# A gated windowed attention kernel: first loads over two queues, idle transposes at the outset, transposes placed beside maxima, last reciprocals placed one tile earlier

## The chip, the cores and the metric

The kernel runs on one core of one Trainium2 chip. The metric is the device time of one execution in microseconds; of several runs the median counts. Five engines share the work: TensorE (PE in the profile, its weight loads PEld), VectorE (DVE), ScalarE (ACT), GpSimd (POOL) and SyncE (SP), which here only issues DMA transfers. ScalarE issues DMA too. Each engine takes its instructions in order and waits on semaphores for the others.

## The reference

For 8 batches of 1024 tokens with 512 features: a layer norm, a windowed attention with 16 heads of 32 features, a gate from a layer of signs, and a residual sum.

```python
xn = _layernorm(x)
q, k, v = proj(xn, Wq, bq), proj(xn, Wk, bk), proj(xn, Wv, bv)
scores = q @ k^T / sqrt(32)
im = arange(1024) % 256
scores = where(im[:, None] >= im[None, :], scores, -1e30)
s = softmax(scores) @ v @ Wo^T + bo
w = (weights >= 0) * 2 - 1
g = silu(clip((xn @ w^T) * scale + bias, -100, 100))
out = x + s * g
```

The lines from `q, k, v` on are shortened; all is float32.

## The kernel before

The tokens are loaded in an order in which the four windows alternate (`tokens`, L127), so that a tile of 128 tokens holds 32 places of each window. The mask is then triangular over tiles, and about half of all tiles of scores is left out.

The work goes by batch `b` and by group `g` of four heads. One group takes nine steps (`NQ`), and a step has two score quads, each four PSUM banks wide, that share one buffer. `probs_quad` (L571) writes scores with keys in rows (lines L577, L588, L599), less the maximum of each query, and ScalarE makes probabilities of them (L612). `maxima_quad` (L494) writes scores of the next group with queries in rows (L501, L515), and VectorE takes maxima of them (L528). Between the two quads TensorE is given other work to fill its time: in the place after a `probs_quad` it also multiplies the last step's probabilities with the values (`attend_quad`, L625). POOL adds probabilities up over tiles (`add_probs`, L643); TensorE sums them over keys (`sum_keys`, L666, or at the end `sum_quad`, L687), ScalarE copies the sums (L661), and VectorE takes reciprocals, 128 columns at a time (`invert`, L700), and multiplies (`normalise_heads`, L704).

The filling work is projections (`product`, L339 to L371, whose matmuls are all L351: q, k, v and the output o), gate tiles (`gate_work`, y_ps, L426 to L449), and turns: transposes by TensorE, four 128x128 blocks into one PSUM bank, which ScalarE or VectorE then copies out. Turned are the normalised tokens of the next batch (`turn` in `norm_work`, L313 to L324), the weights (`turn_weight`, L241; wo's are turned in the third group of the first batch, by words `W` of `OPENING`), and the maxima (`shift_rows`, L552). Products and turns share two PSUM banks (`bank`, L121). An open product holds one of the two until its last chunk is copied out.

The order is planned by hand-written strings (`STEADY`, `OPENING`, `CLOSING`, L787 to L804), one word for each piece, made into `Work` items with costs in microseconds and a test of whether they are ready. `Beside.fill` (L919) takes from this list in each of two places of a step, as much as the place wants: after the score quad of the probabilities up to about 1.2, and after the maxima's up to 2.35 or 2.45 or an even share. Work marked `turn` is allowed once in a place (`turns=1`) or not at all, and is put at the place's end (`edge`). The loop over steps is L1053 to L1140.

At the outset (L154 to L175) all loads are issued: four token tiles of the first batch on SyncE's queue, wk in two halves of 512 KB and three biases on ScalarE's, then four more token tiles, wq, wv, the signs' weights, three rows and wo on SyncE's. The loads share eight semaphores in rotation, so from the ninth on each is issued only when the one eight before it has landed. L993 to L1027 follow: 24 idle transposes into a bank that nobody reads, the turns of wk with four copies by ScalarE, the bias turned, statistics (L285, L286), scale (POOL, L292, L293), normalisation (L305) and turns of four token tiles, the first product of k, constants and statistics of four more tiles on VectorE, wq's turns and the first product of q.

At the end (L1143 to L1162) the output tiles 4, 5, 6, 7, 0, 1, 2, 3 of the last batch are made. Each takes 16 matmuls (L351), two operations of VectorE (L722, L723), one of POOL (L724) and a store. For tiles 0 to 3 a reciprocal and a product of VectorE come first. The last tile goes by `last_output` (L733).

Of the kernel before, what the change touches and what calls it, by code (L numbers as in the profile page):

```python
# [9 lines left out]
F32 = mybir.dt.float32  # L10
# [6 lines left out]
P = 128  # L17
B = 8
L = 1024
D = 512  # L20
# [3 lines left out]
NT = L // P  # L24
NC = D // P
NH = P // DK
# [47 lines left out]
def tile_gated_window_attention(  # L74
# [16 lines left out]
    nc = tc.nc  # L91
# [35 lines left out]
    def tokens(a, b, it):  # L127
        return a[b].rearrange("(w m) d -> m w d", w=NW)[it * MT : (it + 1) * MT]
# [1 line left out]

    xt = {}

    def load_x(b, it):

        where, tag = (vpool, "v") if (b, it // 4) == (0, 1) else (xpool, "x")
        t = where.tile([P, D], F32, tag=tag, name=f"x_{b}_{it}")
        nc.sync.dma_start(t, tokens(x, b, it))
        xt[b, it] = t


    staged = {}

    def fetch_weight(name, src, tiles, queue):

        staged[name] = [t[:, o, :] for t in tiles for o in range(t.shape[1])]
        n = D // len(tiles)
        for i, t in enumerate(tiles):
            queue.dma_start(t, src[i * n : (i + 1) * n, :].rearrange("(o p) d -> p o d", p=P))

    def chunks(where, tag, name):  # L150
        t = where.tile([P, NC, D], F32, tag=tag, name=name)
        return [t[:, 0:2, :], t[:, 2:4, :]]

    for it in range(4):  # L154
        load_x(0, it)
    fetch_weight("wk", wk, chunks(probs, "p", "wk_st"), nc.scalar)
    bias_r = temp("bias_r")[0 : 3 * NC, 0:P]
    for i, src in enumerate((bq, bk, bv)):
        nc.scalar.dma_start(bias_r[i * NC : (i + 1) * NC, :], src.rearrange("(c p) -> c p", p=P))
    bias_c = const.tile([P, 3 * NC], F32, name="bias_c")  # L160
    bq_c, bk_c, bv_c = (bias_c[:, i * NC : (i + 1) * NC] for i in range(3))
    for it in range(4, NT):
        load_x(0, it)
    fetch_weight("wq", wq, chunks(probs, "p", "wq_st"), nc.sync)
    fetch_weight("wv", wv, chunks(total, "total1", "wv_st"), nc.sync)
    fetch_weight("fw", fw, chunks(total, "total0", "fw_st"), nc.sync)
    rows = {}
    for name, src in (("fscale", fscale), ("fbias", fbias), ("bo", bo)):
        t = const.tile([P, D], F32, name=f"{name}_r")
# [1 line left out]
        rows[name] = t  # L171
    fetch_weight(
        "wo", wo,
        [heads.tile([P, 1, D], F32, tag="a0", name=f"wo_st_{o}") for o in range(NC)], nc.sync,
    )  # L175


# [50 lines left out]
            self.early = False  # L228


    wT = {}
    copies = [0]

    def evacuate(dst, src):
# [6 lines left out]
    def turn_weight(name):  # L241


        def turn(c):
            if c == 0:
                wT[name] = const.tile(
                    [P, NC, D], F32R if name == "fw" else F32, name=f"{name}T"
                )
            dst = wT[name]
            if name == "wk" and c % 2:  # L250

                ps = ps_a.tile([P, 512], F32, tag="av", name=f"wkT_{c}")
            else:
                ps = bank(f"{name}T_{c}")
            for o in range(NC):
                nc.tensor.transpose(
                    ps[:, o * P : (o + 1) * P], staged[name][o][:, c * P : (c + 1) * P], ident
                )
            if name == "fw":

                sg = temp(f"sign_{c}")
                nc.vector.tensor_scalar(sg, ps, 0.0, 2.0, ALU.is_ge, ALU.mult)
                nc.vector.tensor_scalar(dst[:, c, :], sg, -1.0, None, ALU.add)
            elif name == "wo":

                nc.scalar.mul(dst[:, c, :], ps, 0.5)
            elif name == "wk":
                nc.scalar.copy(dst[:, c, :], ps)
            else:
                evacuate(dst[:, c, :], ps)  # L270

        return [lambda c=c: turn(c) for c in range(NC)]


    xnT, scaled, normed, turned = {}, set(), set(), set()

    def norm_work(b, half):
        its = range(4 * half, 4 * half + 4)
# [484 lines left out]
    def row_work():  # L763

        wide = []

        def spread():
            wide.append(temp("bvb").rearrange("p (c t) -> p c t", c=NC))
            nc.vector.tensor_copy(wide[0], bv_c.unsqueeze(2).to_broadcast([P, NC, P]))

        def after(ps):
            nc.vector.scalar_tensor_tensor(rows["bo"], rows["bo"], 0.5, ps, ALU.mult, ALU.add)

        return spread, product(
            "bo_ps", [(lambda c=c: (wide[0][:, c, :], wT["wo"][:, c, :])) for c in range(NC)], 0.86, after,
            lambda: bool(wide), True,
        )


# [14 lines left out]
        "V2 G0 V3 V4 G1 V5 V7 V6 G2 k20 q21 k21",  # L794
        "G3 q20 q30 N0 k30 | G4 q31 G5 k31 G6 V0'",
        "G7 N1 V1' | k00' q00' W0 V2' W1 V3' W2 q01' W3",
        "k01' G0' R | q11' k10' G1' k11' q10'",
    )
    CLOSING = (
        "V4 V5 | q20 V7 V6 k20 q21 k21",  # L800
# [24 lines left out]
    def plan(b, g, text):  # L825
        for word in text.split():
            kind, number = word[0], word.strip("'")[1:]
            bb = b + word.count("'")
            i = len(blocks)
            if kind == "|":  # L830
                for block in blocks:
                    block.early = block.early or block.at == (b, g)
                continue
            if kind == "N":
                half = int(number)
                stats, scale, normalise, turn = norm_work(b + 1, half)
                for k in range(4):
                    done = lambda key=(b + 1, 4 * half + k): key in normed
                    there = lambda key=(b + 1, 4 * half + k): key in xt
                    link(  # L840
                        i - 5 + (2 + k // 2 if half else 0) + k // 2,
                        Work(0, stats[k], late=True, ready=there),
                    )
                    by = lambda key=(b + 1, half): key in scaled
                    link(i + half + max(1, k), Work(0, normalise[k], ready=by))
                    link(i + half + 2 + k, Work(0.5, turn[k], turn=True, ready=done))
                link(i - 2 + 2 * half, Work(0, scale, late=True, ready=there))
                continue
            if kind == "-":
                main = []  # L850
            elif kind in "qk":
                main = heads_work(bb, int(number[0]), int(number[1]), kind)
            elif kind == "V":
                main = values_work(bb, int(number))
            elif kind == "W":
                main = [Work(0.5, turn_weight("wo")[int(number)], edge=True)]
            elif kind == "R":
                spread, main = row_work()
                link(i - 3, spread)
            elif kind == "O":  # L860
                fetch, main = output_work(b - 1, int(number))
                link(i - 1, fetch)
            else:
                split, main, squash, finish = gate_work(bb, int(number), kind == "H")
                if split is not None:
                    link(i - 3, split)
                later = 1 if b in (0, B - 1) else 0
                link(i + 2 + later, squash)
                link(i + 3 + later, finish)
            blocks.append(Block((b, g), main))  # L870
# [28 lines left out]
    class Beside:  # L899
# [12 lines left out]
        def closes_slowly(self, want):  # L912
            for w in self.work:
                want -= w.cost
                if w.slow or want < 0:
                    return w.slow and want > -0.1
            return False

        def fill(self, want, kept=None, early=False, turns=1):  # L919

# [69 lines left out]

    norms = [norm_work(0, half) for half in range(2)]

    warm = bank("warm")  # L993
    for _ in range(24):
        nc.tensor.transpose(warm[:, 0:P], ident, ident)
    for fn in turn_weight("wk"):
        fn()
    ps = bank("bias_ps")
    nc.tensor.transpose(ps[:, 0 : 3 * NC], bias_r, ident[0 : 3 * NC, 0 : 3 * NC])
    nc.scalar.copy(bias_c, ps[:, 0 : 3 * NC])  # L1000
    stats, scale, normalise, turn = norms[0]
    for k in range(0, 4, 2):
        stats[k]()
        stats[k + 1]()
        scale(k, k + 2)
        normalise[k]()
        normalise[k + 1]()
    for k in range(4):
        turn[k]()
    for w in heads_work(0, 0, 0, "k"):  # L1010
        w.run()
    more_constants()
# [41 lines left out]
    for s, (b, g, n) in enumerate(steps):  # L1054
# [69 lines left out]
        spent = now.fill(1e9) if n == NQ - 1 else 0.0  # L1124
        if nxt:
            want = max(share, 2.45 if len(S_QUADS[n]) > 1 else 2.35) - spent
            want -= fill(want)
            if want > 0.5:

                want -= fill(want, turns=2)  # L1130
# [18 lines left out]
    for i, it in enumerate(order):  # L1149
        if i + 1 < NT:  # L1150
            units[order[i + 1]][0]()
        if it < 4:
            invert(b, g, 0, it)
            normalise_heads(b, g, 0, it)
        if it == order[-1]:
            rest()
            continue
        if it == order[-2]:
            ahead, rest = last_output(b, order[-1])
            ahead()  # L1160
        for w in units[it][1]:
            w.run()  # L1162
# [45 lines left out]
```

## Time and profile before

| | |
|---|---|
| median of 3 runs | 2244.93 us |
| lowest and highest | 2244.49 and 2246.09 us |
| the profiled execution | 2248.59 us |
| its span, first to last instruction | 2246.7 us |
| mean granted clock of TensorE | 0.996 |
| busy share: TensorE, VectorE, ScalarE, POOL | 98%, 57%, 39%, 59% |
| DMA | 93.55 MB, 42 GB/s over the span |

The span is cut in 40 slices on the page; TensorE is busy 90% or more in all but the first and the last. The DMA engines move 164 GB/s in the first slice and 16 or less in the next two. The chain of work that ended last is followed back from the last instruction to 2176.07 us, so it covers the end alone; TensorE's waits and the order of time show the rest. "Busy" of TensorE counts a matmul at half clock as much as one at full clock, since it lasts longer; the granted clock stands beside it. A row in order of time gives start, duration, engine, line, operation, tiles and shapes, the number of instructions merged in it, and in brackets how long the engine was idle before and for what. Matmuls follow each other before the earlier one has ended, so differences of starts tell more than durations; the 32 matmuls of a product are 16 of the program in two passes each.

### The profile page before, as it was taken

Reading aid. Unit: us, or ns where it says so; the run is one execution under the profiler, and the core shown is the slowest. Engines: PE = TensorE matmul, PEld = TensorE weight load, DVE = VectorE, ACT = ScalarE, POOL = GpSimd, SP = SyncE. Lnnn points to the kernel's source line nnn. Section 1 sums busy time; section 2 is a strip of 40 time slices with the busy share of each in tenths; the row PEclk is TensorE's granted clock in tenths of the full one; section 3 lists DMA queues with packets and bytes.
Section 4 is the critical chain, followed back from the end, with each engine's and each line's share of the span. In section 5 each row is a group of like instructions: output and inputs, shape, how many; then the busy total and the mean of one; then the engine's idle time right before and its main releaser. Section 6 shows DMA issues by size and latency. Waiting matters only on the chain. (4 is left out here: it accounts for less than half of the span.)

```text
span 2246.7 us, 56396 instructions
## 1 busy us (share of the span) xinstructions
PE 2196.6 (98%) x25553; PEld 851.8 (38%) x25553; DVE 1276.6 (57%) x1633; ACT 876.5 (39%) x864; POOL 1323.7 (59%) x1198
## 2 busy tenths in 40 slices
PE   8999999999999999999999999999999999999998
PEld 3334333343333433333333333334333343333333
DVE  4556556665556655566555665565655665555664
ACT  2235433434334434344333443334334344333331
POOL 1256566666566666576556665557666566655562
PEclk9999999999999999999999999999999999999999
DMA  4001000120001210012000120002100111000113
GB/s 164 1 16 34 11 6 29 53 76 30 25 25 39 72 33 25 25 62 68 16 25 25 62 67 16 25 26 66 62 16 27 41 62 62 7 20 25 44 53 123
DMA packets 49672, 93.55 MB, mean 42 GB/s; under 512 B 5388, under 2 KB 5656, under 8 KB 49432
## 3 DMA queue, kind: packets, MB, share of 16 engines
q1 hardware_dynamic: 48720, 88.76, 12.0%
q8 instruction: 200, 3.28, 0.6%
q10 hardware_dynamic: 712, 1.19, 0.2%
q14 instruction: 40, 0.33, 0.0%
HBM read 56.37 MB, written 33.55 MB: 40 GB/s over the span
## 5 line engine op out<-in xcount | busy, mean ns | idle before, releaser
L643 POOL TENSOR_TENSOR p<-p,p 128x512 f32<-128x512 f32 x930 | 1096.4, 1212 | 202.7 <-PE av L625 111.2
L528 DVE TENSOR_REDUCE pm<-s 128x4 f32<-128x2048 f32 (+3 forms) x384 | 664.9, 1752 | 608.8 <-PE s L515 605.9
L612 ACT ACTIVATE p<-t 128x2048 f32<-128x2048 f32 x288 | 540.9, 1878 | 856.4 <-PE t L599 797.8
L700 DVE RECIPROCAL aT<-aT 128x128 f32<-128x128 f32 x256 | 230.2, 928 | 222.4 <-ACT aT L661 222.4
L515 PE MATMUL s<-k,q 32*128 32x512 f32 (+3 forms) x3072 | 320.2, 510 | 7.8 <-ACT p L612 6.9
L625 PE MATMUL av<-p,v 128*32 128x512 f32 (+3 forms) x3072 | 308.2, 496 | 1.6 <-DVE aT L704 1.4
L599 PE MATMUL t<-q,k 32*128 32x512 f32 (+3 forms) x3072 | 306.1, 492 | 0.0
L351 PE MATMUL q_ps<-xnT,wqT 128*32 128x512 f32 (+2 forms) x2656 | 254.2, 497 | 5.5 <-ACT xnT L322 4.7
L351 PE MATMUL k_ps<-xnT,wkT 128*32 128x512 f32 (+2 forms) x2784 | 257.2, 487 | 1.1 <-ACT xnT L322 0.7
L351 PE MATMUL v_ps<-wvT,xnT 128*32 128x512 f32 (+3 forms) x2712 | 254.9, 491 | 0.0
L351 PE MATMUL o_ps<-woT,aT 128*32 128x512 f32 (+2 forms) x2584 | 244.6, 501 | 1.7 <-ACT xnT L322 0.7
L724 POOL TENSOR_TENSOR s<-s,xb 128x512 f32<-128x512 f32 x63 | 85.8, 1362 | 245.3 <-DVE s L723 245.3
L428 POOL TENSOR_SCALAR y<-y 128x512 f32<-128x512 f32 x64 | 39.6, 619 | 279.9 <-DVE y L427 265.2
L422 POOL TENSOR_TENSOR x<-xnT,x 128x512 fp32r<-128x512 f32 x58 | 74.0, 1277 | 166.4 <-ACT x L421 164.0
L599 PEld LDWEIGHTS t<-q,k 32*128 32x128 f32 x3072 | 139.1, 185 | 25.8
L351 PEld LDWEIGHTS k_ps<-xnT,wkT 128*32 128x32 f32 x2784 | 82.7, 110 | 170.4 <-issue 142.5
L351 PEld LDWEIGHTS q_ps<-xnT,wqT 128*32 128x32 f32 x2656 | 78.3, 109 | 177.3 <-issue 152.5
L625 PEld LDWEIGHTS av<-p,v 128*32 128x32 f32 x3072 | 70.3, 108 | 195.9 <-issue 163.4
L351 PEld LDWEIGHTS v_ps<-wvT,xnT 128*32 128x32 f32 x2712 | 78.6, 109 | 167.8 <-issue 143.9
L515 PEld LDWEIGHTS s<-k,q 32*128 32x128 f32 x3072 | 116.3, 185 | 59.4 <-ACT p L612 47.5
L449 PE MATMUL y_ps<-fwT,x 128*128 128x512 f32 x464 | 135.5, 418 | 1.7 <-ACT k L394 1.3
L351 PEld LDWEIGHTS o_ps<-woT,aT 128*32 128x32 f32 x2584 | 76.2, 109 | 156.7 <-issue 135.2
(95 smaller groups left out, 1465.2 us busy)
## 6 DMA issues: line engine op xcount, KB each, us to landing
x<-in_L_attn_x_dram SPq DMA_DIRECT2D x64, 256.0 KB, 3.2
g<-t SPq DMA_DIRECT2D x64, 256.0 KB, 2.0
gb<-g SPq DMA_DIRECT2D x64, 256.0 KB, 3.1
xb<-in_L_attn_x_dram SPq DMA_DIRECT2D x64, 256.0 KB, 3.1
out_dram<-s SPq DMA_DIRECT2D x63, 256.0 KB, 2.5
wk_st<-in_L_attn_Wk_dram ACTq DMA_DIRECT2D x2, 512.0 KB, 5.5
wq_st<-in_L_attn_Wq_dram SPq DMA_DIRECT2D x2, 512.0 KB, 4.6
wv_st<-in_L_attn_Wv_dram SPq DMA_DIRECT2D x2, 512.0 KB, 6.4
```

Source lines behind the costliest of these rows:

```text
L351: nc.tensor.matmul(hold[0][cols, lo:hi], lhsT=lhsT[:, cols], rhs=rhs[:, lo:hi], start=(i == 0 and lo == 0), stop=(i == n - 1), skip_group_ ...
L422: nc.gpsimd.tensor_tensor(part[1], src, part[0].bitcast(F32), ALU.subtract)
L428: nc.gpsimd.tensor_scalar(y[0], y[0], MAX_VAL, -MAX_VAL, ALU.min, ALU.max)
L449: nc.tensor.matmul(hold[0], lhsT=part[i][:, c, :], rhs=wT["fw"][:, c, :], start=(i == 0 and c == 0), stop=(i == 1 and c == NC - 1),)
L515: nc.tensor.matmul(sc[:, h, at : at + w], lhsT=qt[b, g][head_rows(h), i * P : (i + 1) * P], rhs=kt[b, g][head_rows(h), lo:hi], start=not f ...
L528: nc.vector.tensor_reduce(pm[:, 0 if lo == 0 else 1, i, :], sc[:, :, at : at + w], AX.X, ALU.max)
L599: nc.tensor.matmul(sc[:, h, at : at + w], lhsT=kt[b, g][head_rows(h), j * P : (j + 1) * P], rhs=qt[b, g][head_rows(h), q0 : q0 + w], start ...
L612: nc.scalar.activation(pt[:, :, :width], sc[:, :, :width], AF.Exp, scale=SCALE)
L625: nc.tensor.matmul(av[b, g, f][head_rows(h), lo : lo + w], lhsT=vt[b, j][:, g * P + h * DK : g * P + (h + 1) * DK], rhs=pts[b, g, n][:, h, ...
L643: nc.gpsimd.tensor_tensor(t[:, hs, lo : lo + w], t[:, hs, lo : lo + w], p[:, hs, at : at + w], ALU.add)
L700: nc.vector.reciprocal(r, r)
L724: nc.gpsimd.tensor_tensor(s, s, xr, ALU.add)
```

## The change

There are five parts.

- First loads: token tiles 0 and 2 go on SyncE's queue and 1 and 3 on ScalarE's, then one half of wk on each; the three biases go on SyncE's queue. In SyncE's order the half of wk and the biases stand ahead of token tiles 4 to 7.
- Outset on the engines: 44 idle transposes instead of 24, into a bank of another pool, and four more after each turned token tile. The four turns of wk go to the four banks of the score quad, so no copy has to come between them; two copies are ScalarE's and two VectorE's. In the built program the first copy waits for all 16 transposes, and VectorE's first for ScalarE's second. All four statistics come before the four normalisations on VectorE, and the bias is turned after the tokens.
- Turns of wo are marked `turn` instead of `edge`. The row work `R` (bo_ps) moves four words later and waits until wo's turns have been issued.
- `turn_ahead`: right after a score quad for maxima, a turn that is ready is issued first, when the first piece of work in the list that is not ready comes within 2.4 us; no other turn goes into that place's first filling.
- End: reciprocal and product of the next output tile among 0 to 3 are issued before the tile at hand.

In the built program's order, apart from the outset and the end, the pieces are rearranged from the third group of the first batch to the first group of the second batch: TensorE's and ScalarE's there, three pieces of VectorE's (bvb's copy, reciprocals, bo_r), and four places of POOL's. After that five places differ: in batches 2 to 6 of 0 to 7, in the third group, the turn of token tile 7 and the last chunk of output tile 3 change places. The number of turns, products and DMA transfers is the same.

```diff
-    def load_x(b, it):
+    def load_x(b, it, queue=nc.sync):
...
-        nc.sync.dma_start(t, tokens(x, b, it))
+        queue.dma_start(t, tokens(x, b, it))
...
-            queue.dma_start(t, src[i * n : (i + 1) * n, :].rearrange("(o p) d -> p o d", p=P))
+            queues[i % len(queues)].dma_start(t, src[i * n : (i + 1) * n, :].rearrange("(o p) d -> p o d", p=P))
...
-        load_x(0, it)
-    fetch_weight("wk", wk, chunks(probs, "p", "wk_st"), nc.scalar)
+        load_x(0, it, (nc.sync, nc.scalar)[it % 2])
+    fetch_weight("wk", wk, chunks(probs, "p", "wk_st"), [nc.sync, nc.scalar])
...
-        nc.scalar.dma_start(bias_r[i * NC : (i + 1) * NC, :], src.rearrange("(c p) -> c p", p=P))
+        nc.sync.dma_start(bias_r[i * NC : (i + 1) * NC, :], src.rearrange("(c p) -> c p", p=P))
...
-            if name == "wk" and c % 2:
-                ps = ps_a.tile([P, 512], F32, tag="av", name=f"wkT_{c}")
+            if name == "wk":
+                if c == 0:
+                    staged["quad"] = ps_q.tile([P, NH, 512], F32, tag="quad", name="wkT")
+                ps = staged["quad"][:, c, :]
...
                 nc.scalar.mul(dst[:, c, :], ps, 0.5)
+                turned.add(("wo", c))
             elif name == "wk":
-                nc.scalar.copy(dst[:, c, :], ps)
+                staged["copy", c] = lambda: (
+                    nc.vector.tensor_copy(dst[:, c, :], ps) if c > 1
+                    else nc.scalar.copy(dst[:, c, :], ps)
+                )
...
-            lambda: bool(wide), True,
+            lambda: bool(wide) and all(("wo", c) in turned for c in range(NC)), True,
...
-        "k01' G0' R | q11' k10' G1' k11' q10'",
+        "k01' G0' | q11' k10' R G1' k11' q10'",
...
-                main = [Work(0.5, turn_weight("wo")[int(number)], edge=True)]
+                main = [Work(0.5, turn_weight("wo")[int(number)], turn=True)]
...
+        def turn_ahead(self):
+            i = next((i for i, w in enumerate(self.work) if w.turn), None)
+            if i is None or not self.work[i].ready():
+                return 0
+            cost = 0.0
+            for w in self.work:
+                cost += 0 if w.turn else w.cost
+                if cost > 2.4:
+                    return 0
+                if w.cost and not w.ready():
+                    w = self.work.pop(i)
+                    w.run()
+                    return w.cost
+            return 0
...
-    warm = bank("warm")
-    for _ in range(24):
-        nc.tensor.transpose(warm[:, 0:P], ident, ident)
+    warm = ps_a.tile([P, 512], F32, tag="av", name="warm")
+
+    def idle_turns(n):
+        for _ in range(n):
+            nc.tensor.transpose(warm[:, 0:P], ident, ident)
+
+    idle_turns(44)
     for fn in turn_weight("wk"):
         fn()
-    ps = bank("bias_ps")
+    stats, scale, normalise, turn = norms[0]
+    for k in range(4):
+        stats[k]()
+        if k % 2:
+            scale(k - 1, k + 1)
+    for k in range(4):
+        normalise[k]()
+    staged["copy", 0]()
+    for k in range(4):
+        turn[k]()
+        idle_turns(4)
+        if k == 1:
+            staged["copy", 1]()
+    staged["copy", 2]()
+    staged["copy", 3]()
+    ps = ps_a.tile([P, 512], F32, tag="av", name="bias_ps")
     nc.tensor.transpose(ps[:, 0 : 3 * NC], bias_r, ident[0 : 3 * NC, 0 : 3 * NC])
     nc.scalar.copy(bias_c, ps[:, 0 : 3 * NC])
-    stats, scale, normalise, turn = norms[0]
-    for k in range(0, 4, 2):
-        stats[k]()
-        stats[k + 1]()
-        scale(k, k + 2)
-        normalise[k]()
-        normalise[k + 1]()
-    for k in range(4):
-        turn[k]()
...
             want = max(share, 2.45 if len(S_QUADS[n]) > 1 else 2.35) - spent
-            want -= fill(want)
+            turned_now = now.turn_ahead()
+            want -= turned_now
+            want -= fill(want, turns=0 if turned_now else 1)
...
-        if it < 4:
-            invert(b, g, 0, it)
-            normalise_heads(b, g, 0, it)
+        if i + 1 < NT and order[i + 1] < 4:
+            invert(b, g, 0, order[i + 1])
+            normalise_heads(b, g, 0, order[i + 1])
```

## The prediction on record

> **What bounds the kernel now.** I read the page's busy shares first, then the clock and the engines in stretches, the waits of TensorE, the order of time at four places, and the chain that ended last. All times are on the span's clock.
>
> ```profile
> PE 2196.6 (98%) x25553; PEld 851.8 (38%) x25553; DVE 1276.6 (57%) x1633; ACT 876.5 (39%) x864; POOL 1323.7 (59%) x1198
> ```
>
> TensorE is busy for 2196.6 of 2246.7 us, so 50 us is all that can be won without taking work away. A wait of TensorE costs its length, and a matmul at half clock its length again. The change touches four places where TensorE stands still or runs slowly.
>
> The first is the outset. Stretches of 3.4 us (busy time and count of each engine, then the granted clock, DMA share and GB/s):
>
> ```profile
> 5.01:8.42 3.41, 2.80 (x25) 2.43 (x23) 1.76 (x4) 1.04 (x1) 0.36 (x3) 1.00 1.05 394
> 8.42:11.84 3.42, 1.17 (x10) 0.99 (x9) 2.54 (x6) 2.71 (x7) 0.73 (x1) 1.00 0.99 361
> 11.84:15.25 3.41, 1.80 (x10) 1.57 (x8) 2.23 (x9) 1.31 (x3) 0.94 (x2) 0.50 1.04 374
> 15.25:18.66 3.41, 2.73 (x14) 0.59 (x16) 2.98 (x8) 0.69 (x2) 1.13 (x3) 0.50 1.05 398
> 18.66:22.07 3.41, 3.41 (x20) 0.79 (x16) 0.00 (x0) 0.00 (x0) 0.73 (x2) 0.50 0.95 317
> 22.07:25.49 3.42, 2.93 (x24) 1.68 (x16) 1.36 (x3) 1.27 (x2) 0.00 (x0) 1.00 1.05 396
> ```
>
> The reader sees the clock fall to 0.50 after a stretch with 1.17 us of matmul and rise again only after a full one. So the first product runs slowly, as two rows of TensorE in order of time show:
>
> ```profile
> 16.26 6.50 PE L351 MATMUL k_ps<-xnT,wkT 128*32 128x512 f32 x32 [0.68 <-ACT xnT L322]
> 25.57 3.64 PE L351 MATMUL q_ps<-xnT,wqT 128*32 128x512 f32 x32
> ```
>
> Both are the same 32 matmuls. DMA moves about 390 GB/s throughout: transfers are limited by rate here.
>
> The second and third are turns (transposes) with their evacuation on ScalarE right behind them. From TensorE's waits (total, times, longest), then one batch in order of time:
>
> ```profile
> PE q_ps L351 <- ACT xnT L322: 4.7, 7, 0.7
> ...
> PE woT L256 <- ACT xnT L322: 1.2, 1, 1.2
> ```
> ```profile
> 816.92 1.06 PE L351 MATMUL o_ps<-woT,aT 128*32 128x512 f32 x8
> 817.07 2.29 DVE L528 TENSOR_REDUCE pm<-s 128x4 f32<-128x2048 f32 x1 [2.28 <-PE s L515]
> 817.92 0.66 PE L321 MATMUL xnT_ps<-ident,x 128*128 128x128 f32 x4
> 818.61 0.58 ACT L322 COPY xnT<-xnT_ps 128x512 f32<-128x512 f32 x1 [2.08 <-PE xnT_ps L321]
> 819.25 1.39 PE L351 MATMUL q_ps<-xnT,wqT 128*32 128x512 f32 x16 [0.68 <-ACT xnT L322]
> ```
>
> The product q_ps needs the turn just ahead of it, and waits 0.68 us. The same rows stand at 1090.53, 1361.8, 1633.33 and 1904.62. The fourth place is the end, in the chain of waits:
>
> ```profile
> 2228.12 0.69 DVE s L723
> 2228.82 0.87 DVE aT L700
> 2229.69 0.02 issue
> 2229.71 0.30 DVE aT L704
> 2230.01 0.04 issue
> 2230.06 1.11 PE o_ps L351 x8
> ```
>
> Each of the last output tiles waits for a reciprocal and a product that VectorE takes up only after the tile before.
>
> **The change part by part.** The profiled execution took 2248.59 us for a span of 2246.7; the median of the runs shown is 2244.93. I sum against the span and take the result off both.
>
> *Outset.* The ten first loads change queues. x1 and x3 go to ScalarE's queue, one half of wk and three bias loads to SyncE's, the latter ahead of x4 to x7 and wq. At 390 GB/s from about 2.6 us, x0 to x3 and wk (2 MB) need 5.2 us, plus 0.6 for landing: the last of wk lands at 8.4 us, where the second half now releases its transpose at 6.78. Tokens come earlier, x0 and x1 by about 4.5 (now 5.06 and 7.10). VectorE then needs 4 x 0.87 for statistics, POOL 1.1 and VectorE 4 x 0.54 to normalise: done by 10.
> The 24 idle transposes took 4.61 us, 0.21 each up to 5.0 and 0.11 after. The 20 more add 2.2 us and end at 8.0, still ahead of wk: free. The 16 of wk (14 took 1.75) end at 10.2. All of their copies wait for the last of the 16, where the first now starts at 8.67, so this part is later than now. From 10.1 TensorE does four blocks of four turns and four idle ones, 0.9 each; the fourth turn ends at 13.4, its copy (0.58) at 14.1. ScalarE's six copies of 0.55 from 10.4 would be done at 13.7, so the idle turns cost some 0.5. The product starts at 14.2, not 16.26: **2.1**. TensorE has no gap over 0.5 us from 1.3 to 14.2, so I expect the clock to stay at 1.00 and the product to take 3.6, not 6.50: **2.8**. Next are wq's turns at 17.7. SyncE's loads rotate over eight semaphores, so each waits for the eighth before it: wq's halves now wait for wk's second half and the first bias. With issue at 9 to 10 and 4.6 us to land they are there by 14.6. VectorE has taken over two of wk's copies (2 x 0.69) and ends the statistics of x4 to x7 at 18.5 as now (18.37), which costs 0.2 at wq's first copy. Sum **4.7**.
> A section of the Trainium skill (TensorE: Matmul & The Clock Gate, Part 4: PE-mode transpose) says that transposes don't count as busy for the clock. By that the product would stay slow; this trace disagrees, as transposes alone went from 0.21 to 0.11 us at 5.0.
> The Trainium skill (DMA: Bandwidth & Descriptors, Issuing engines are not separate DMA queues) says that loads from two engines share the same DMA engines. The 390 GB/s agree: what tokens gain, wk loses.
>
> *Weight turns of the first batch.* Turns of wo become "turn" work, so no two stand in one place unless asked for, and one turn may go right after a score quad. Five or six steps near 240 to 340 us are reordered. Gone: waits of 0.27 and 1.22 (x4's turn and wo's side by side), 0.12, and 0.68 at 271.78, 2.3 in all. New: x7's turn stands behind the exponential of its step, whose 1.88 us its copy must wait out, so q_ps stands 1.3 where the next score quad would have waited 0.4 anyway: -0.9. VectorE gets two reciprocals and a 0.42 copy ahead of a maximum that had no slack: -0.9. On POOL, y of the second gate tile is ready about 1 us sooner against its queue, so the exponential of 327.57, which waited for POOL, loses some 0.7 of its wait of 1.1: +0.7. The two steps with adjacent turns last 8.8 and 7.8 us from score quad to score quad (starts at 241.88, 250.66, 258.43), where 7.1 would do (the exponential ends 3.4 after the start, the quad takes 1.1, the maximum and its hand-over 2.6): 2.4, of which 1.6 are the waits named; I add 0.5 of the same kind for the steps from 273.96 to 289.3 (7.6 and 7.8): +1.3. Sum **2.5**, bounds -1 (the stalls come, the slack doesn't) and 4.
>
> *Turns in the steady batches.* In five batches the turn of x7 moves ahead of the output chunk in the rows shown. From 816.92: 0.13 until the turn begins, 0.59 to the next work (as at 265.2, from turn to score quad), 0.86 for the chunk, 1.32 for q_ps: the score quad starts at 819.82, not at 820.57. Gain **0.75**, five times **3.7**. ScalarE's copy has 0.86 us for its 0.58. The maximum ends at 819.36, so nothing later than that holds the quad. The turn needs a PSUM bank, mT's, which ScalarE frees at 816.52: 0.5 to spare. Bounds: 0 (another wait takes it) and 5 x 1.1 (the maximum alone decides).
>
> *End.* Reciprocal and product of the next tile come before the two VectorE operations of this one: 0.87 + 0.30 leave the chain three times, and TensorE's chunks of 0.86 (3.43 a tile) take over. Of 3.80 a tile, 3.43 stay: 3 x 0.37, **1.1**. VectorE has 2.6 of work in 3.43. What is late next is x's last tile on SyncE's queue, issued after the same product on VectorE (2236.55, 3.01 us), so all behind it moves as it does. Bounds 0.4 and 1.6.
>
> 4.7 + 2.5 + 3.7 + 1.1 = 12.0: span 2234.7, this execution 2236.6, median **2232.9**.
>
> **The rivals.**
> *Given back.* The saved matmul time of the middle and the steady batches is lost at the next wait for POOL (0.92 us in each batch near 785, where an exponential waits for a probability buffer). For it: the exponentials start late there. Against: POOL stands idle for 5 to 9 us twice between 806 and 851, so it follows TensorE. Gain 4.7 + 1.1: 2239.1.
> *The clock falls all the same.* Idle turns don't hold it: 2.8 stays lost, the gain is 9.2: 2235.7. Against: transposes alone brought the rate from 0.21 to 0.11. The Trainium skill's rule on transposes, above, would give this case.
> *Slower.* One mechanism: wq. The three biases, on SyncE now, stand ahead of x4 to x7 and gate wq's second half through the rotation. On ScalarE's queue the second and third were issued only at 4.38 and 7.09. TensorE loses a microsecond for each that wq lands after 17.7; the kernel gets slower from a landing at 29.7 on, and at 35 it takes 2250. It landed in 4.6 us, so this is far off.
> *It doesn't do what it says.* The turns move, yet maxima hold each quad, and wk's later landing eats the outset: 2243, no change.
>
> **How the numbers follow.** Forecast 0.70, given back 0.13, clock 0.10, no effect 0.04, slower 0.03. The forecast's own bounds: the outset 3 to 6, the middle 0 to 4, the batches 2.5 to 4.5, the end 0.7 to 1.4; not all err together, so 9 to 15 off the median, 2230 to 2236. The range takes in the clock case and most of the given-back one: 2229.5 to 2239. Two executions can be told apart from about 0.2%, 4.5 us: faster 0.93, same 0.04, slower 0.03.
>
> **What would show it.** Right: clock 1.00 from 5 to 25 us, the first k_ps at 14.2 and 3.6 long; no wait of q_ps for xnT of 0.7 at the five places and the next score quad 0.7 sooner; no wait of wo's turn; 3.4 us a tile in the last chain. Wrong: a wait of wk's transposes beyond 8.4, of wqT for its load, of score quads for POOL by more than now, or q_ps behind an exponential for more than 1.3 us.

## The result and the profile after

The changed kernel takes **2236.43 us** (median of 6 runs, 2234.68 to 2237.02), the kernel before 2245.57 (6 runs, 2244.49 to 2246.5): a ratio of **0.9958**, interval 0.9946 to 0.9971. It is faster, by 9.1 us where 12.0 were forecast, and 3.5 above the forecast of 2232.9. The profiled execution took 2235.59 for a span of 2233.8, 12.9 less than the profiled one before. Two parts of that 12.9 are events of single executions and not of the change: a gate tile that landed late near 706 us (1.5, by the score quads at 711.51 and 720.38), and a stretch of half clock from 2179.29 to 2182.71 us (1.4). Both lie where the change moves nothing, and kernels with the change had them too in the experiments below: the same two steps were longer by 1.6 in e2 and 1.3 in e10, and e3 and e8 had a stretch of half clock near the same place.

To see where the rest lies, I took the starts of all 288 score quads (t, L577 before, L583 after) from both traces and noted where their distance grows:

| stretch | gained in the profiles | forecast |
|---|---|---|
| up to the first score quad (80.08 and 77.33 us) | 2.75 | 4.7 |
| first batch, third and fourth group (341.25 and 335.60) | 2.90 | 2.5 |
| five steady places (0.88 each) | 4.41 | 3.7 |
| executions' own differences | 3.0 | - |
| last score quad to the end (42.3 and 42.5) | -0.2 | 1.1 |

The page's first row, after. TensorE is busy for 2.9 us less, although 36 idle transposes were added:

```profile
PE 2193.7 (98%) x25605; PEld 856.5 (38%) x25605; DVE 1277.3 (57%) x1635; ACT 875.0 (39%) x862; POOL 1324.1 (59%) x1198
```

The outset, after, in the same stretches (busy time and count of each engine, clock, DMA share, GB/s):

```profile
5.01:8.42 3.41, 3.41 (x29) 3.31 (x27) 1.13 (x5) 0.00 (x0) 1.08 (x4) 1.00 0.90 317
8.42:11.84 3.42, 1.36 (x13) 1.22 (x12) 2.75 (x7) 0.00 (x0) 1.28 (x2) 1.00 0.74 252
11.84:15.25 3.41, 3.41 (x33) 3.41 (x32) 0.92 (x3) 2.39 (x5) 0.00 (x0) 1.00 0.90 306
```

The clock is 1.00 throughout, as forecast, but DMA moves 317, 252 and 306 GB/s where it moved 394, 361 and 374. TensorE in order of time, after:

```profile
10.62 1.97 PE L258 MATMUL wkT<-ident,wk_st 128*128 128x128 f32 x16 [2.06 <-DMA wk_st<-in_L_attn_Wk_dram]
...
16.32 3.64 PE L357 MATMUL k_ps<-xnT,wkT 128*32 128x512 f32 x32
```

The product takes 3.64 instead of 6.50, but starts at 16.32 (before 16.26): TensorE stood 2.06 us for wk, which came at 10.6 and not at 8.4. All of the 2.75 is clock. From wk's last share (10.57) to the product it took 5.75 us.

A steady place, after (third group of the third batch; the rows shown of before begin at 816.92), rows of weight loads and of VectorE left out, and what is left of TensorE's wait for xnT (total, times, longest):

```profile
809.70 0.66 PE L327 MATMUL xnT_ps<-ident,x 128*128 128x128 f32 x4
810.29 1.06 PE L357 MATMUL o_ps<-woT,aT 128*32 128x512 f32 x8
810.39 0.59 ACT L328 COPY xnT<-xnT_ps 128x512 f32<-128x512 f32 x1 [1.08 <-PE xnT_ps L327]
811.17 1.37 PE L357 MATMUL q_ps<-xnT,wqT 128*32 128x512 f32 x16
...
812.47 0.40 PE L583 MATMUL t<-shift,neg 3*128 3x384 bf16 x8
```
```profile
PE q_ps L357 <- ACT xnT L328: 1.0, 2, 0.7
```

The copy now runs beside the output chunk, and q_ps follows without a wait; the total for xnT falls from 4.7 in seven waits to 1.0 in two. The wait of woT for xnT (1.2) is gone from the list.

The chain of waits at the end, after (here and below, rows of issue and of less than 0.1 us are left out):

```profile
2213.97 0.71 DVE o_ps L728
2214.70 0.70 DVE s L729
2215.42 4.89 DMA xb<-in_L_attn_x_dram
2220.44 1.29 POOL s L730
2221.75 0.60 SPq L731
2222.39 3.00 DMA gb<-g
```

No reciprocal is in it any more. TensorE's last matmul starts 32.85 us after the last score quad, not 35.38. But the end stands where it stood, because the gate of the last tile (gb) is loaded late: its buffer is that of an earlier x tile, and it stands on SyncE's queue behind the store of that tile (L731), which waits for POOL, which waits for x (xb).

### The profile page after: what moved, and what is told of

Same layout as the page of the kernel before. It is cut to its first block, busy times and chain, and to the rows that moved or that the text cites. A ratio compares the mean times of both kernels' runs of the same rounds, so it can differ in the third digit from the quotient of the medians.

```text
span 2233.8 us, 56503 instructions
## 1 busy us (share of the span) xinstructions
PE 2193.7 (98%) x25605; PEld 856.5 (38%) x25605; DVE 1277.3 (57%) x1635; ACT 875.0 (39%) x862; POOL 1324.1 (59%) x1198
```

## The experiments

Twelve kernels ran. In the four groups that ran together (e1 to e4, e5 to e8, e9 to e11, e12) the kernel before took 2245.54, 2245.55, 2245.46 and 2246.03. "Product" is the start of the first k_ps in the profile, "end" the time from the last score quad to the end.

| run | median (range, runs) | ratio to before | product | end |
|---|---|---|---|---|
| before | see above | 1 | 16.26 | 42.3 |
| changed | 2236.43 (2234.68-2237.02, 6) | 0.9958 [0.9946, 0.9971] | 16.32 | 42.5 |
| e1 | 2243.20 (2242.47-2246.23, 11) | 0.9991 [0.9982, 1.0] | 15.96 | 42.4 |
| e2 | 2237.03 (2236.28-2238.73, 5) | 0.9962 [0.9948, 0.9976] | 16.78 | 41.8 |
| e3 | 2234.74 (2234.04-2235.64, 5) | 0.9952 [0.9939, 0.9964] | 14.45 | 41.7 |
| e4 | 2241.53 (2240.9-2243.4, 11) | 0.9983 [0.9974, 0.9991] | 18.58 | 42.3 |
| e5 | 2231.76 (2230.21-2234.91, 5) | 0.9940 [0.9928, 0.9953] | 16.46 | 38.8 |
| e6 | 2234.55 (2233.65-2237.06, 5) | 0.9954 [0.9941, 0.9966] | 16.17 | 40.7 |
| e7 | 2236.27 (2234.92-2236.65, 5) | 0.9959 [0.9946, 0.9971] | 18.14 | 41.5 |
| e8 | 2237.86 (2235.35-2240.94, 5) | 0.9965 [0.9951, 0.9978] | 19.26 | 41.7 |
| e9 | 2238.84 (2238.0-2241.63, 8) | 0.9972 [0.9962, 0.9982] | 16.22 | 43.6 |
| e10 | 2235.48 (2233.88-2237.51, 5) | 0.9954 [0.9941, 0.9968] | 13.60 | 41.6 |
| e11 | 2230.94 (2229.47-2232.7, 5) | 0.9933 [0.992, 0.9945] | 14.15 | 37.8 |
| e12 | 2233.39 (2233.18-2234.46, 5) | 0.9944 [0.993, 0.9958] | 14.44 | 41.7 |

My theory after the result: idle transposes gave all of the outset's gain; the new loads gave nothing and the end little, for reasons of their own; the turns gave what they should. Rivals: the loads keep the clock; the steady gain is given back elsewhere; the end is bound by POOL and stores whatever is done.

**e1, idle transposes alone**, on the kernel before:

```diff
-    warm = bank("warm")
-    for _ in range(24):
-        nc.tensor.transpose(warm[:, 0:P], ident, ident)
...
+    idle_turns(44)
...
         turn[k]()
+        idle_turns(4)
```

> The kernel before, with 44 idle transposes instead of 24 and four more after each turned token tile (into a bank of the score quad), and nothing else of the change. Theory: idle transposes alone keep the granted clock at 1.00 through the first products, so that k_ps takes 3.6 us instead of 6.50 wherever it starts; its start is set by the landings and by ScalarE's copies and stays at 16.3 to 16.8. Then q_ps starts near 23 instead of 25.57, and the kernel is about 2.5 us faster than before (2243). Rival: the changed kernel keeps its clock because its loads let TensorE's real work stand closer together; then the clock falls here as before, the idle turns cost up to 0.5, and the time is 2245.5 to 2246.

```profile
15.96 3.64 PE L351 MATMUL k_ps<-xnT,wkT 128*32 128x512 f32 x32 [0.24 <-ACT xnT L322]
```

The clock stays at 1.00, k_ps takes 3.64, q_ps starts at 22.41 and the first score quad at 76.91, 3.2 sooner than before and 0.4 sooner than in the changed kernel. The median is 2.3 below that of before; its interval just reaches 1. So the outset's gain can be had without any of the new loads.

**e2, the changed kernel without them**:

```diff
-    idle_turns(44)
+    idle_turns(24)
...
         turn[k]()
-        idle_turns(4)
```

> The changed kernel with 24 idle transposes as before and none between the turns of tokens. Theory (idle transposes hold the clock): the granted clock falls to 0.50 during the first product, k_ps takes up to 6.5 us, and the kernel is 2 to 3 us slower than the changed one: 2238.5 to 2239.5. Rival (loads and order hold it): the clock stays at 1.00, k_ps even starts some 0.4 us sooner than 16.32 since ScalarE's copies and no idle turns set it: 2236.

The clock did fall, but only 0.7 was lost (0.6 in the medians, less than their ranges), which neither theory had said. Stretches of e2, cut where its clock changes:

```profile
7.74:11.16 3.42, 1.91 (x9) 1.91 (x10) 2.17 (x6) 0.00 (x0) 1.28 (x2) 0.50 0.87 295
11.16:14.57 3.41, 3.41 (x18) 3.19 (x17) 0.00 (x0) 1.17 (x2) 0.00 (x0) 0.50 0.98 333
14.57:17.98 3.41, 2.59 (x22) 1.31 (x25) 2.16 (x7) 2.13 (x5) 0.00 (x0) 1.00 1.01 356
```

The low stretch lies on the wait for wk and on turns, and the product behind it runs at 1.00. In the middle row TensorE does nothing but transposes, and the clock rises after it. So these transposes, fp32 blocks of 128x128 by an identity, do raise the clock, against the rule weighed in the prediction (the Trainium skill, TensorE: Matmul & The Clock Gate, Part 4: PE-mode transpose).

**e3, the changed kernel with the loads of before**:

```diff
-        load_x(0, it, (nc.sync, nc.scalar)[it % 2])
-    fetch_weight("wk", wk, chunks(probs, "p", "wk_st"), [nc.sync, nc.scalar])
+        load_x(0, it)
+    fetch_weight("wk", wk, chunks(probs, "p", "wk_st"), [nc.scalar])
...
-        nc.sync.dma_start(bias_r[i * NC : (i + 1) * NC, :], src.rearrange("(c p) -> c p", p=P))
+        nc.scalar.dma_start(bias_r[i * NC : (i + 1) * NC, :], src.rearrange("(c p) -> c p", p=P))
```

> The changed kernel with the first loads of before: all token tiles on SyncE's queue, both halves of wk and the biases on ScalarE's. Theory: the new loads are a loss, since wk, which everything on TensorE waits for at 10.6, landed at 6.7 before, and the tokens that come earlier only wait. Then wk's turns start behind the idle ones at 8.6, the token tiles are normalised by 11.5 to 12, the first product starts at about 13.5 instead of 16.3, and the kernel is 2 to 3 us faster than the changed one: 2233.5 to 2234.5. Rival: tokens first is what counts; x_3 lands at 8.4 instead of 5.1, the turns of tokens come later than wk's and the product starts at 16 or later: 2236 to 2238.

The product starts at 14.45, the first score quad 1.9 sooner than in the changed kernel, and the median is 1.7 below. The new loads are a loss, though the product came 0.9 later than I expected: wk's turns waited for the 44 idle ones (8.80), and ScalarE's copies followed.

**e4, no turn ahead**:

```diff
-            turned_now = now.turn_ahead()
+            turned_now = 0
```

> The changed kernel in which no turn is put right behind a score quad ahead of the other work (the test for it always answers no); everything else stays, the turns of wo too. Theory: the five steady places lose their 0.86 us each and the product waits 0.68 for its copy again: 4.3 slower than the changed kernel, up to 1 more or less from the one place of the first batch that moves with it: 2240 to 2241.5. Rival (given back at waits for POOL): the steady batches follow another engine, and the time moves by less than 1: 2236 to 2237.

At each of the five places the score quad falls back by 0.88, 4.4 in all, and TensorE's waits have the old row again:

```profile
PE q_ps L357 <- ACT xnT L328: 4.4, 7, 0.7
```

The median is 5.1 above the changed kernel's. "Given back" is out. The outset of e4 is the same program as in the changed kernel, but the product started at 18.58, not 16.32: the new loads also vary from one execution to the next.

**e5 and e6, loads of the last output tile issued early**, into two buffers of the values' pool; e6 has the reciprocals at their old place as well:

```diff
-            g = xres.tile([P, D], F32, tag="io", name=f"gb_{b}_{it}")
+            where, tag = (vpool, "v") if (b, it) == (B - 1, 3) else (xres, "io")
+            g = where.tile([P, D], F32, tag=tag, name=f"gb_{b}_{it}")
...
     units[4][0]()
+    units[3][0]()
     for i, it in enumerate(order):
-        if i + 1 < NT:
+        if i + 1 < NT and order[i + 1] != 3:
             units[order[i + 1]][0]()
```

> The changed kernel in which the two loads for the last output tile (gate and x) go into buffers of the values' pool that are free by then, and are issued before the loop over the last eight tiles instead of after the sixth of them. Theory: the reciprocals that were moved up did free TensorE (its last matmul starts 32.7 to 32.9 us after the last score quad, 35.4 before), but the last tile then waits for its two loads, which need buffers and stand behind a store on SyncE's queue, so the end came only 0 to 0.7 sooner. Without that wait the end follows TensorE: 37 to 38 us from the last score quad to the end instead of 41.7 to 42.5, and the kernel is 4 to 5 us faster than the changed one: 2231.5 to 2232.5. Rival: the POOL operations of the last two tiles and the stores set the end in any case: at most 1 us, 2235.5 to 2236.5.

> The same early loads of the last tile, with reciprocal and product of the tiles 0 to 3 at their old place, right before their own tile. Theory: TensorE's last matmul starts 35.4 after the last score quad again, and the end follows it by 4.5 to 5: 39.5 to 40.5, some 2.5 later than with the reciprocals moved up: 2234 to 2235. Rival (the moved reciprocals are worth nothing whatever follows): the same time as the run with early loads and moved reciprocals, within 0.5.

e5 is 4.7 below the changed kernel, e6 2.8 above e5, both times as the theory said; the ends, 38.8 and 40.7, came later than the 37 to 38 and 39.5 to 40.5 expected. The intervals of the two ratios overlap, so the traces have to tell e5 from e6: TensorE's last matmul starts 32.70 after the last score quad in e5 and 35.38 in e6. The last parts of the chain of waits, e5 first, then e6:

```profile
2215.62 4.21 DMA xb<-in_L_attn_x_dram
2219.97 1.28 POOL s L731
2221.24 1.24 POOL s L746
2222.57 1.29 POOL xb L747
2223.88 0.44 DVE s L764
```
```profile
2222.67 0.69 DVE s L730
2223.36 0.87 DVE aT L706
2224.25 0.30 DVE aT L710
2224.60 2.41 PE o_ps L756 x40
```

In e6 reciprocal and product stand ahead of TensorE's last part; in e5 they are gone, and what is late is x of the last tile but two, with two POOL operations of the last tile queued behind it. In this end the moved reciprocals are worth 1.9 in the profiles (40.7 against 38.8) and 2.8 in the medians; in the change itself, where the last loads hold the end, less: the end took 42.3, 42.4 and 43.6 in the three profiles with the old end, and 41.5 to 42.5 in the eight with the changed one (medians 42.4 and 41.7).

**e7, e8 and e12, which part of the loads does it.** e7 puts the biases back on ScalarE's queue; e8 both halves of wk and the biases (tokens on two queues); e12 has all tokens on SyncE's queue, wk's first half on ScalarE's and the second on SyncE's:

```diff
# e7
-        nc.sync.dma_start(bias_r[i * NC : (i + 1) * NC, :], src.rearrange("(c p) -> c p", p=P))
+        nc.scalar.dma_start(bias_r[i * NC : (i + 1) * NC, :], src.rearrange("(c p) -> c p", p=P))
# e8, beside that of e7
-    fetch_weight("wk", wk, chunks(probs, "p", "wk_st"), [nc.sync, nc.scalar])
+    fetch_weight("wk", wk, chunks(probs, "p", "wk_st"), [nc.scalar])
# e12
-        load_x(0, it, (nc.sync, nc.scalar)[it % 2])
-    fetch_weight("wk", wk, chunks(probs, "p", "wk_st"), [nc.sync, nc.scalar])
+        load_x(0, it)
+    fetch_weight("wk", wk, chunks(probs, "p", "wk_st"), [nc.scalar, nc.sync])
```

> The changed kernel with the three bias loads back on ScalarE's queue, behind its half of wk. Theory A: the biases on SyncE's queue and the rotation of semaphores behind them are what lets the transfers run thin (250 to 317 GB/s from 5 to 15 us, and a last DMA engine up to 2.5 us behind the first); then wk lands by 9, all 16 shares of a load within 0.6 us, and the first product starts at 14.5 to 15. Theory B: splitting tokens and wk over two queues does it; then wk still lands at 9.2 to 11.4 with shares up to 2.5 us apart, and the product starts at 16 to 18.6 as in the changed kernel. Time 2234.5 to 2235.5 by A, 2236 to 2237 by B.

> The changed kernel with the four token tiles on two queues as it has them, and both halves of wk and the biases behind x1 and x3 on ScalarE's queue. By 390 GB/s, 1 MB of tokens and 1 MB of wk need 5.2 us from 2.6, and x4 and x5 on SyncE's queue share the rate: wk lands by about 9.5. Theory A (biases on SyncE's queue are the trouble): shares of a load land within 0.6 us, wk by 9.5 and the first product starts at about 15. Theory B (tokens split over two queues): shares land up to 2.5 apart, wk at 10 to 11, the product at 16 or later. Either way later than with the loads of before (14.45), since wk is what TensorE waits for.

> The changed kernel with all four token tiles of the outset on SyncE's queue, wk's first half alone on ScalarE's and its second half on SyncE's behind the tokens, the biases behind it as in the change. It tells which split spreads the shares of a load: so far they spread (up to 2.8 us between first and last) in six of seven profiles with the tokens on two queues, with wk on one queue or two, with the biases on either, and in none of four with tokens on SyncE's queue and wk on ScalarE's. Theory: it is the tokens on two queues; then all shares land within 0.6 us here, wk is there by 8.5, the first product starts at 14 to 14.7, and the time is 2234 to 2235.5. Rival: it is wk's halves on two queues or the biases between tokens; then shares of x2 to x5 or of wk's second half lie 1.5 us or more apart, the product starts after 15.5: 2236 to 2237.5.

Each load reports to its semaphore in 16 shares. First and last share of x2 and of the later half of wk, in us:

| profile | tokens, wk on queues | x2 | wk, later half |
|---|---|---|---|
| before | one, one | 7.38-7.76 | 6.04-6.73 |
| e3 | one, one | 7.57-7.81 | 6.44-6.80 |
| e12 | one, two | 6.08-6.88 | 8.12-8.92 |
| changed | two, two | 5.53-8.32 | 8.24-10.57 |
| e2 (same loads) | two, two | 5.62-6.10 | 8.31-9.21 |
| e4 (same loads) | two, two | 4.82-6.91 | 8.22-11.38 |
| e7 | two, two | 4.94-5.37 | 9.07-10.94 |
| e8 | two, one | 5.56-7.56 | 9.85-12.06 |

e7 and e8 went by their theories B: the products started at 18.14 and 19.26. With tokens on two queues the first shares come sooner, but the last of wk's come 1.9 to 3.2 after the first, in all profiles but e2, and TensorE waits for the last one. (In e4 x3 spread over 3.3 and one half of wk over 3.6, so the "up to 2.8" in the expectation is too low.) With tokens on one queue the spread of x0 to x3 and wk is at most 0.95 in all seven profiles, wherever wk and the biases go, and in e12 the product starts at 14.44. The 0.6 expected of e12 was too low, and its time, 2233.39, is 0.6 below the range expected. So the biases are cleared, and wk's split too; wide spreads came only with the tokens on two queues, though not each time (e2). Two stretches of e12, in which DMA moves 391 and 333 GB/s where the changed kernel had 317 and 252:

```profile
5.00:8.42 3.42, 3.11 (x29) 2.87 (x27) 3.09 (x7) 0.00 (x0) 1.09 (x4) 1.00 1.05 391
8.42:11.84 3.42, 2.88 (x26) 2.88 (x27) 2.08 (x6) 1.07 (x2) 1.28 (x2) 1.00 1.02 333
```

Why some shares lag stays open: the packets show which queue they came by, not which of the 16 engines moved them. Nor do the runs tell the two queues apart from the pace of issue: with the tokens on two queues the sixth large load was issued at 2.33 us, with one at 2.82 (e3) to 3.38 (e12).

**e9, the turns alone** on the kernel before (wo's marks, the row work, `turn_ahead`; outset, loads and end as before):

> The kernel before with the two middle parts of the change alone: turns of wo marked as turns, the row work moved and made to wait, and a turn put right behind a score quad. Outset, loads and end as before. Theory (each part does its own work): the middle gains 2.9 and the five steady places 0.86 each, 4.3, as in the trace of the changed kernel: 7.2 in all, 2238 to 2239. Rival (part of that was the outset's, whose shift moved the waits for DMA and POOL): 4 to 6, 2239.5 to 2241.5.

6.6 in the medians. In the profile the middle gains 2.93 (2.90 in the changed kernel) and the five places 0.88 each: these parts stand on their own.

**e10, loads of before and no extra idle transposes**: the edits of e2 and e3 together.

> The changed kernel with the first loads of before, 24 idle transposes and none between the turns: what is left of the change at the outset is the order of statistics, wk's copies and the bias. Theory (idle transposes hold the clock, where loads don't keep TensorE standing in any case): the granted clock falls to 0.50 somewhere between 8 and 20 us and the first product or wk's turns run at half speed; 1.5 to 3 slower than with the old loads and all idle transposes (2234.74): 2236.3 to 2237.7. Rival (as the run without idle transposes on the new loads showed 0.7 only): the low stretch falls on waiting time, less than 1: 2234.5 to 2235.7.

The theory failed here: the clock did not fall in the profiled execution, and the product started at 13.60, 0.85 sooner than with the idle transposes (e3).

```profile
8.42:11.84 3.42, 1.28 (x11) 0.91 (x10) 2.75 (x8) 1.90 (x5) 2.01 (x3) 1.00 1.03 353
11.84:15.25 3.41, 2.86 (x25) 1.45 (x29) 3.05 (x10) 1.67 (x5) 0.00 (x0) 1.00 0.98 320
```

In the medians e10 is 0.7 slower than e3, with a range of 3.6 against 1.6. A clock that falls in some executions and not in others would look like that. The mean granted clock over a whole run says something of this: in e10 it was 0.997 in the slowest run and 0.999 in the two fastest, in e3 0.998 or 0.999. At 0.997 at least 11 us went by at half clock, where the profiled execution had 4.2, all at its end. So executions did differ in this, but whether at the outset is not shown.

The theory that the idle transposes gave all of the outset's gain falls with this run. They are enough to hold the clock (e1), but with the old loads the new order did without them in this profile: its first score quad stands at 74.68, sooner than in any other (75.44 in e3, 80.08 before).

**e11, what the runs point to**: e3's loads, e5's early loads, wk's first copies ahead of the tokens', and fewer idle transposes:

```diff
-    idle_turns(44)
+    idle_turns(32)
     for fn in turn_weight("wk"):
         fn()
+    staged["copy", 0]()
+    staged["copy", 1]()
+    idle_turns(12)
...
-    staged["copy", 0]()
     for k in range(4):
         turn[k]()
-        idle_turns(4)
-        if k == 1:
-            staged["copy", 1]()
+        idle_turns(2)
```

> The changed kernel with the first loads of before, wk's turns after 32 idle transposes and its two copies by ScalarE ahead of the tokens' copies, 12 idle transposes behind wk's turns and two instead of four between the tokens' turns, and the last output tile's two loads issued early into buffers of the values' pool. By the theories so far the gains add up: old loads 1.7 to 1.9, copies of wk off ScalarE's path and fewer idle transposes 1.0 (first product at 13.4 instead of 14.45), early loads of the last tile 4.7: 2228.5 to 2229.5. Rival: fewer idle transposes let the clock fall in the first product, 2 to 3 more: 2231 to 2232.5.

The fastest of all, 14.5 below before and 5.5 below the changed kernel, but 1.4 to 2.4 above what I expected. The product started at 14.15, not 13.4: the 12 idle transposes behind wk's held the first token's turn until 10.89, when its tile had been ready since 10.1. The end (37.8) is as expected. Besides, of the 2.2 by which its first score quad came sooner than the changed kernel's, 1.2 were gone by the last: five steps are longer by about 0.25, the same five as in e3. Why is open.

## Why the prediction came out as it did

- *Outset, 4.7: the step that failed.* "At 390 GB/s ... the last of wk lands at 8.4": it landed at 10.57, and in the other profiles of these loads at 9.2 to 11.4. I had taken the rate of one layout of queues for that of another. The 2.1 for the earlier start was 0; what follows wk was priced right, 5.8 from its landing to the product against 5.75. The 2.8 for the clock was right in size (2.75 in all), but by luck. Its reason, no gap over 0.5 us, was not right: there was one of 2.06, and the clock stayed at 1.00 all the same (last section). Nor can the 2.8 be won in every execution: in 5 of the 51 runs of the kernel before that ran beside the experiments the mean granted clock was 0.999 or 1.000 (2243.5 to 2244.8 us, the others 2244.8 to 2248.3), too high for the 10 us at half clock that the profile shows at the outset.
- *Middle, 2.5*: 2.90, and 2.93 alone (e9). The waits named are gone from the list between 240 and 343 us: 1.2 for woT and 1.1 for the exponential; that of q_ps is 0.3 instead of 0.7.
- *Steady batches, 3.7*: 4.41. The mechanism was right; each place gave 0.88 and not 0.75, since the score quad followed 2.77 after the turn (809.70 to 812.47), as forecast, but the turn began 0.1 sooner.
- *End, 1.1: the second step that failed.* -0.2 in this pair of profiles, 0.7 by the medians of all. TensorE was freed by 2.5, more than I counted. The prediction named the load that would be late next and then let it "move as it does"; it does not move, since its buffer and its place behind a store tie it to POOL and to an earlier load (e5, e6).
- *Sum.* With the terms as they came, 2.75 + 2.90 + 4.41 - 0.2 = 9.9, near the 9.1 of the medians. The two failed steps fell short by 3.2, and the other two terms came out 1.1 higher than forecast; that they made up for a third of it was luck too. The 12.9 between the two profiled executions holds 3 us that the change did not make.
- *Rivals.* Given back: excluded (e4, e9). The clock falls all the same: not in this execution, but in e4, with the same outset, it did from 11.96 to 15.37. The measured 2236.4 lies nearer to this rival's 2235.7 than to the forecast, though its mechanism was not at work in the profile: the time alone would have pointed to the wrong cause. Slower through wq: no, its turns started 2.8 sooner than before.

## What to carry to other kernels

Before loads are reordered to bring one thing sooner, find what the first long wait stands on: here all work waited for the last share of wk, and tokens that came sooner only waited for it. When a chain is cut, follow the next one to its buffers and its queue: the moved reciprocals were worth 1.9 to 2.8 us, but only once two loads could be issued early. And price steps by places in the trace that recur, not by one execution's total: the five places repeated within 0.01 us, while the total differed by 3 us through events of its own.

## What the runs showed of the hardware

- The clock follows windows that run freely. All changes of the granted clock within one profile lie whole multiples of 3.413 us apart: before, 11.84 and 2244.15 us are 654.0 of them apart, in e4 11.96 and 2234.03 are 651.0. Cut into these windows, the clock at the outset fell after windows in which TensorE was busy for 0.89 (e7), 0.97 (e4), 1.16 (before, e8), 1.17 (e9) and 1.29 us (e2), and stayed after 1.55 (e6), 1.67 (e5) and more. By this the gap of 2.06 us did no harm in the changed kernel since it fell into two windows: counted back from its change at 2227.95, a window ends at 9.28, in the midst of the gap:

```profile
5.87:9.28 3.41, 2.69 (x25) 2.45 (x23) 1.13 (x5) 0.00 (x0) 0.97 (x2) 1.00 0.85 307
9.28:12.70 3.42, 2.08 (x19) 2.08 (x20) 2.63 (x6) 0.08 (x1) 1.28 (x2) 1.00 0.75 237
```

  The Trainium skill (TensorE: Matmul & The Clock Gate, Part 1: The HAM clock gate) tells of such free windows; these traces agree, with 3.413 us.
- Busy time is no full account of the fall. Late in the kernel before, a window with 1.86 us busy (up to 2179.29) was followed by half clock, where the windows of transposes above with less were not. In all 14 profiles the clock fell after every window with 1.37 us or less and after none with 2.07 or more; between them both happened, and what decides there is open. Nor is one long gap needed: in e8 the clock fell at 473.63 after a window with 2.06 us busy in which no gap was longer than 0.7 us.
- The rise asks for more. The clock stayed low after windows with 1.80 and 2.73 us busy (before) and 2.49 (e9), and rose after 2.82 (before, up to 2182.71), 2.89 (e9, up to 4.23), 2.98 (e2, up to 4.33) and every fuller one. At 4.23 and 4.33 the spacing of the idle transposes goes from 0.21 to 0.11 us.
- A load's 16 shares can land 2 to 3.6 us apart while DMA as a whole moves well under what it moved with another split of the same loads (252 to 317 GB/s in the changed kernel, 333 and 391 in e12).
